# A graph layer's edge loop: shares of a column copy between ScalarE and VectorE, its rates, and where a row is added

## The chip, the cores and the metric

One core of a Trainium2 chip. The metric is the device time of one execution in microseconds (us). Engines are named as the profile names them: PE is TensorE (PEld its weight loads), DVE is VectorE, ACT is ScalarE, POOL is GpSimd, SP is the engine that issues most DMAs.

## What is computed

A message-passing layer over N = 12500 nodes with 64 features and E = 200000 edges with 32 features, a residual and a layer norm. Edges are sorted by destination, and low node numbers have many more edges than high ones.

```python
msg_in = concat([x[src], x[dst], edge_attr])            # 64 + 64 + 32
messages = relu(msg_in @ mW1 + mb1) @ mW2 + mb2          # hidden 128
aggregated = segment_sum(messages, dst, num_segments=N)
upd = relu(concat([x, aggregated]) @ uW1 + ub1) @ uW2 + ub2
out = layernorm(x + upd)
```

All of it is float32.

## The kernel before

**Tables.** The part of the first product that belongs to a node is computed once a node: `tab_a` holds x @ mW1[:64] and `tab_b` x @ mW1[64:128] + mb1, 128 numbers a node. An edge's hidden row is then the sum of a row of `tab_a` (its source), a row of `tab_b` (its destination) and a small product of its 32 features.

**Tiles and groups.** 128 edges make a tile, six tiles a group (`SUB = 6`): 1563 tiles, 261 groups, the last of three tiles. Two groups share their selection matrices (`SUP = 12`). The main loop runs over the groups `s` and writes each engine's order by hand; an engine works its own instructions off in that order and waits on semaphores for the others. In one pass of the loop stand, among others: `node_part(s)`, a first part of the DVE copies (`joined`), `collect(s - 1)`, in every other pass `select` (lines 257 and 263, the selection matrices) with another part of the copies, `edge_part(s + 1)`, the last part of the DVE copies, and the ACT copies (`singly`).

**What a group needs.**
- GpSimd gathers the source rows: one indirect DMA a tile (line 223) from `tab_a` into the tile `xg`. The first ten groups gather rows of `x` itself, which are transposed. `ROWB = 9` buffers let the gathers of a group start once a group nine places earlier has been added.
- PE computes the destinations' and the edge features' part into the PSUM tile `pc` (line 385, `edge_part`).
- DVE adds the gathered rows to `pc` (line 408; line 411 for the last, shorter group), and ACT applies the Relu, from `pc` into the SBUF tile `h` (line 409; 412).
- PE sums `h` by destination into the PSUM tile `sums` and counts edges into `cnt` (lines 444 and 441, `collect`).
- Some 480 nodes at a time are closed, updated, normalised and stored: lines 447 to 537, spread over several passes. `cps`, `y`, `ss`, `sd`, `hTu` and `pu` are their tiles.

**Copied groups.** A gather of one tile takes GpSimd as long as any other, so in some groups the last two tiles are not gathered. Their 256 source columns are copied instead, out of the transposed node features that lie in SBUF (`xtop` and `xbot`), as 128 columns of `xc`, each made of two halves; PE then multiplies `xc` with `w1a` into `pc` (line 388). `ACTS` of the 128 columns are copied by ACT (line 358, one instruction a column), the rest by DVE (line 365). The column's address is data, so each chunk of up to 8 columns is preceded by a load of its addresses into the engine's registers (line 334). `PACE` says how many copied groups are started for each group of the loop, by stage; the list `COPIED` follows from it, and so does the share of columns copied in each pass (`portion`). There are 107 copied groups, and a copied group's add covers four tiles of the six.

Of the kernel before, what the change touches and what calls it, by code (L numbers as in the profile page):

```python
# [12 lines left out]
AF = mybir.ActivationFunctionType  # L13
ALU = mybir.AluOpType
# [10 lines left out]
SUB = 6  # L25
# [45 lines left out]
U8 = mybir.dt.uint8  # L71
YBASE = XBASE + 4 * XCOLS
LEAD = 8
PACE = ((11, 0.435), (50, 0.458), (130, 0.438), (170, 0.425), (261, 0))
FINAL = 258


def progress(s):

    return sum(r * max(0, min(s + 1, b) - a) for (a, r), (b, _) in zip(PACE, PACE[1:]))  # L80


COPIED = []
# [1 line left out]
    while progress(s) >= len(COPIED) + 1 and s + 3 < FINAL:  # L85
        COPIED.append(s + 3)
LAST = 4 * (N - 1)
ACTS, CHUNK = 64, 8


def updates():
# [24 lines left out]
def gnn_kernel(ctx: ExitStack, tc: tile.TileContext, x1T, x, eT, e_rows, src, src_row, dst, dst_row, wlist, wrow, wnext, whalf,  # L116
# [24 lines left out]
    nc = tc.nc  # L141
# [64 lines left out]
    def tiles(s):  # L206
        return range(s * SUB, min((s + 1) * SUB, NT))
# [20 lines left out]
    with tc.tile_pool(name="sup", bufs=2) as sup, tc.tile_pool(name="work", bufs=2) as work, tc.manual_schedule():  # L228
# [140 lines left out]

        def parts(n):  # L370

            return [(slice(b, b + 1), (n - b + 1) // 2) for b in range(2) if n > b]

        def edge_part(s):
# [16 lines left out]
        def node_part(s):  # L391

            n = len(tiles(s))
            pc = pcs.pop(s)
            h = work.tile([P, 2, SUB // 2, DH], F32, name="h")
            if s < XG:
                xt = xs.pop(s)
                for i in range(n):
                    k, b = divmod(i, 2)
                    q = 64 * b  # L400
                    nc.tensor.matmul(pc[:, b, k, :], xt[q:q + 64, k, :], w1a[q:q + 64], start=False,
                                     stop=i + 2 >= n)
                nc.scalar.activation(h, pc, AF.Relu)
            else:
                a = xg.pop(s)[0].rearrange("p (b k) f -> p b k f", b=2)
                if n == SUB:
                    m = SUB // 2 - (s in COPIED)
                    nc.vector.tensor_tensor(pc[:, :, :m], pc[:, :, :m], a[:, :, :m], op=ALU.add)  # L408
                    nc.scalar.activation(h, pc, AF.Relu)  # L409
                for b, m in parts(n) if n < SUB else []:  # L410
                    nc.vector.tensor_tensor(pc[:, b, :m], pc[:, b, :m], a[:, b, :m], op=ALU.add)
                    nc.scalar.activation(h[:, b, :m], pc[:, b, :m], AF.Relu)
            hs[s] = h

        def opened(u):
# [359 lines left out]
        n = UPD[K - 1]  # L775
# [8 lines left out]
        for s in range(last + 2):  # L784
# [13 lines left out]
            if s < NSUB:  # L798
                node_part(s)
                joined(s, 0, 3 if j == 0 and g + 1 < NSUP else 2)  # L800
# [59 lines left out]
    with tc.If(flag > 0), tc.tile_pool(name="gen", bufs=1) as up:  # L860
# [28 lines left out]
        with tc.For_i(0, NT, 1) as t:  # L889
# [26 lines left out]
            pc = psum.tile([P, DH], F32, name="pcg", tag="pc")  # L916
# [4 lines left out]
            h = up.tile([P, DH], F32, name="hg")  # L921
# [6 lines left out]
            m = up.tile([P, 1], F32, name="m")  # L928
# [97 lines left out]
```

## Time and profile before

| | us |
|---|---|
| median of 3 runs | 1726.23 |
| lowest and highest | 1725.64, 1727.5 |
| the profiled execution | 1724.81 |
| its span, first to last instruction | 1723.0 |
| granted TensorE clock, mean | 0.582 of full speed |

Rows of a view that groups instructions read: line, engine, operation, written tile <- read tiles, shape and count, then busy time and mean duration in ns, then the idle time of the engine just before these instructions and what ended it. In a list of waits stand the total in us, the number of times and the longest. "issue" is idle time for which the profile shows no wait: the engine's own sequencer was at something else. In a row of a stage stand start:end, length, the busy time of each engine with its count of instructions, the granted clock, the DMA share and GB/s. A timeline row has its start, its duration, and in brackets the idle time before it.

### The profile page before, as it was taken

To read this page: it belongs to the slowest core of one execution; us is meant where nothing else is said; L and a number is where in the kernel's file an instruction comes from. 1 tells how busy PE (TensorE), PEld (TensorE's weight loads), DVE (VectorE), ACT (ScalarE), POOL (GpSimd) and SP (SyncE) were. 2 spreads that over 40 slices of the span, in tenths; PEclk is the share of its full clock that TensorE was granted. 3 is DMA by queue.
4 is the path that set the end of the run, shared out by engine and by line. 5 is a ranking of instruction groups with operands and counts; after the bars stand their busy time and mean duration, and the time that the engine had idled before them with its cause. 6 is when DMAs were issued, how large, how long until landed. Compare 5 with 4: busy or idle time off the path is not lost. (4 is left out here: it accounts for less than half of the span.)

```text
span 1723.0 us, 47177 instructions
## 1 busy us (share of the span) xinstructions
PE 1444.9 (84%) x9576; PEld 1251.9 (73%) x9608; DVE 1062.7 (62%) x7605; ACT 1555.2 (90%) x7279; POOL 1277.0 (74%) x1358
## 2 busy tenths in 40 slices
PE   2696888888878888888888988888887898999987
PEld 2585777787767777777776887776776677877776
DVE  1426666666666666666666666666666666666563
ACT  0176999999999999999999999999999999999892
POOL 7777777777777777777777777777777777777771
PEclk8575555556555555655565555556666656555576
DMA  8783433433333333333333333343333443334332
GB/s 208 202 182 99 118 109 111 125 101 93 94 95 97 92 101 94 98 102 96 105 98 108 108 109 106 104 112 110 108 104 107 112 111 109 110 107 111 105 108 63
DMA packets 205695, 190.92 MB, mean 111 GB/s; under 512 B 55938, under 2 KB 171862, under 8 KB 205414
## 3 DMA queue, kind: packets, MB, share of 16 engines
q1 hardware_dynamic: 147700, 92.42, 19.6%
q0 software_dynamic: 43168, 86.53, 18.4%
q10 hardware_dynamic: 14546, 8.93, 1.9%
q8 instruction: 91, 1.49, 0.3%
q14 instruction: 190, 1.55, 0.3%
HBM read 170.26 MB, written 17.47 MB: 109 GB/s over the span
## 5 line engine op out<-in xcount | busy, mean ns | idle before, releaser
L223 POOL DMA_INDIRECT xg<-tab_a,src_s x1289 | 1218.4, 945 | 393.1 <-issue 356.1
L358 ACT ACTIVATE xc<-xtop,xbot 128x1 f32 x6848 | 1299.2, 290 | 31.3 <-issue 21.4
L365 DVE TENSOR_TENSOR xc<-xtop,xbot 128x1 int32 x6848 | 584.7, 153 | 451.3 <-issue 440.2
L444 PE MATMUL sums<-sel,h 128*128 128x32 f32 x3126 | 642.9, 372 | 79.3 <-ACT h L409 78.4
L444 PEld LDWEIGHTS sums<-sel,h 128*128 128x128 f32 x3126 | 609.2, 296 | 104.4 <-ACT h L409 89.5
L385 PE MATMUL pc<-rhs,l 64*128 64x128 f32 x3126 | 421.0, 412 | 81.5 <-DVE tb L610 28.8
L385 PEld LDWEIGHTS pc<-rhs,l 64*128 64x128 f32 x3126 | 348.1, 289 | 145.4 <-issue 63.0
L408 DVE TENSOR_TENSOR pc<-pc,xg 128x768 f32<-128x768 f32 (+1 forms) x250 | 212.9, 852 | 76.9 <-PE pc L385 26.7
L409 ACT ACTIVATE h<-pc 128x768 f32<-128x768 f32 x250 | 200.3, 801 | 25.4 <-DVE pc L408 24.5
L257 DVE TENSOR_TENSOR l<-l,cps 128x768 f32<-128x768 int32 (+1 forms) x134 | 126.7, 945 | 28.9 <-DMA l<-in_dst_row 17.5
L441 PEld LDWEIGHTS <-one 128*1 128x1 bf16 x1563 | 57.6, 83 | 84.9 <-issue 74.8
L441 PE MATMUL cnt<-sel,one 128*1 128x32 bf16 x1563 | 94.3, 187 | 0.7 <-issue 0.5
L388 PE MATMUL pc<-w1a,xc 64*128 64x128 f32 x428 | 80.5, 384 | 0.0
L263 DVE TENSOR_TENSOR sel<-cps,drc 128x384 f32<-128x384 f32 x131 | 71.3, 545 | 12.6 <-PE sums L444 12.5
L223 POOL DMA_INDIRECT xg<-in_x,src_s x60 | 57.6, 959 | 19.1 <-issue 18.0
L388 PEld LDWEIGHTS pc<-w1a,xc 64*128 64x128 f32 x428 | 71.5, 298 | 0.0
L482 PE MATMUL pu<-xw,uz 128*128 128x480 f32 (+2 forms) x64 | 61.9, 1071 | 0.3 <-DVE xw L459 0.3
L602 ACT COPY tb<-pb 128x512 f32<-128x512 f32 (+1 forms) x13 | 7.4, 569 | 60.1 <-DMA tab_a<-tb 21.1
L439 PE MATMUL cnt<-zero_b 128*1 128x512 bf16 x32 | 18.5, 578 | 47.1 <-DVE xw L459 42.5
L483 PE MATMUL pu<-sums_s,w2u 128*128 128x480 f32 (+2 forms) x64 | 54.4, 952 | 0.0
L498 PE MATMUL cps<-ux,xw 128*128 128x64 f32 x244 | 45.7, 348 | 8.5 <-DVE sel L263 7.9
L498 PEld LDWEIGHTS cps<-ux,xw 128*128 128x128 f32 x244 | 41.0, 253 | 13.8 <-DVE sel L263 10.3
(111 smaller groups left out, 598.6 us busy)
## 6 DMA issues: line engine op xcount, KB each, us to landing
l<-in_dst_row SPq DMA_DIRECT2D x262, 96.0 KB
l<-in_eT SPq DMA_DIRECT2D x262, 96.0 KB
xg<-tab_a,src_s POOLq DMA_INDIRECT x1289
rhs<-tab_b SPq DMA_DIRECT2D x361, 32.0 KB
tab_b<-tb SPq DMA_DIRECT2D x13, 512.0 KB
rhs<-tab_b SPq DMA_DIRECT2D x387, 16.0 KB
tab_a<-tb ACTq DMA_DIRECT2D x12, 512.0 KB
out<-y SPq DMA_DIRECT2D x30, 128.0 KB
```

The source lines that it names most:

```text
L223: nc.gpsimd.indirect_dma_start(out=a[:, i, :] if s < XG else a[:, i // 2, i % 2, :], out_offset=None, in_=A[:, :] if s >= XG else x[:, :], ...
L257: nc.vector.tensor_tensor(l[r], l[r].bitcast(I32), node[r].unsqueeze(2).broadcast_to([r.stop - r.start, SUP // 2, P]), op=ALU.is_equal)
L263: nc.vector.tensor_tensor(s[:, :nt], slot.unsqueeze(1).broadcast_to([P, nt, WIN]), drc[:, g * SUP:g * SUP + nt].unsqueeze(2).broadcast_to( ...
L358: nc.scalar.activation(o[:, e:e + 1], top.bitcast(F32), AF.Identity, bias=bot.bitcast(F32))
L365: nc.vector.tensor_tensor(o[:, e:e + 1].bitcast(I32), top.bitcast(I32), bot.bitcast(I32), op=ALU.bitwise_or)
L385: nc.tensor.matmul(pc[:, b, k, :], L[g][q:q + 64, m, :], rhs[g % 2][q:q + 64, w, :], start=s >= XG or k == 0, stop=s >= XG and not copied)
L388: nc.tensor.matmul(pc[:, b, k, :], xc[s][q:q + 64], w1a[q:q + 64], start=False, stop=True)
L408: nc.vector.tensor_tensor(pc[:, :, :m], pc[:, :, :m], a[:, :, :m], op=ALU.add)
L409: nc.scalar.activation(h, pc, AF.Relu)
L441: nc.tensor.matmul(pn[:, bass.ds(ws[i], WIN)], one, SB[g][:, k0 + i, :, 1], start=False, stop=ends and i == n - 1)
L444: nc.tensor.matmul(ps[:, bass.ds(ws[i], WIN)], h[:, i % 2, i // 2, :], S[g][:, k0 + i, :], start=False, stop=ends and i == n - 1)
L498: nc.tensor.matmul(py[:, i], xw[u % 2][:, i * P:(i + 1) * P], ux, start=i == 0, stop=False)
```

## The change

Four edits. ACT copies 62 columns of a copied group where it copied 64, and DVE 66 where it copied 64. The four rates of `PACE` become 0.44, 0.462, 0.437 and 0.423 for 0.435, 0.458, 0.438 and 0.425; there are still 107 copied groups, some of them one group earlier. In groups that are not copied DVE writes the sum of `pc` and the gathered rows into `h` in SBUF, and ACT applies the Relu to `h` in place, where the sum was written back to `pc` in PSUM and the Relu read it there; the last, shorter group likewise. Copied groups keep the add in PSUM.

```diff
-PACE = ((11, 0.435), (50, 0.458), (130, 0.438), (170, 0.425), (261, 0))
+PACE = ((11, 0.44), (50, 0.462), (130, 0.437), (170, 0.423), (261, 0))
...
-ACTS, CHUNK = 64, 8
+ACTS, CHUNK = 62, 8
...
         def parts(n):
 
+            if n == SUB:
+                return [(slice(0, 2), SUB // 2)]
             return [(slice(b, b + 1), (n - b + 1) // 2) for b in range(2) if n > b]
...
-                if n == SUB:
-                    m = SUB // 2 - (s in COPIED)
+                if s in COPIED:
+                    m = SUB // 2 - 1
                     nc.vector.tensor_tensor(pc[:, :, :m], pc[:, :, :m], a[:, :, :m], op=ALU.add)
                     nc.scalar.activation(h, pc, AF.Relu)
-                for b, m in parts(n) if n < SUB else []:
-                    nc.vector.tensor_tensor(pc[:, b, :m], pc[:, b, :m], a[:, b, :m], op=ALU.add)
-                    nc.scalar.activation(h[:, b, :m], pc[:, b, :m], AF.Relu)
+                for b, m in parts(n) if s not in COPIED else []:
+                    nc.vector.tensor_tensor(h[:, b, :m], pc[:, b, :m], a[:, b, :m], op=ALU.add)
+                    nc.scalar.activation(h[:, b, :m], h[:, b, :m], AF.Relu)
```

## The prediction

> **What bounds the kernel now.** I read the page's first part, then the waits of GpSimd, then the timelines of GpSimd and VectorE side by side, then busy time by stage, and last the waits inside each stage.
>
> ```profile
> span 1723.0 us, 47177 instructions
> ...
> PE 1444.9 (84%) x9576; PEld 1251.9 (73%) x9608; DVE 1062.7 (62%) x7605; ACT 1555.2 (90%) x7279; POOL 1277.0 (74%) x1358
> ```
>
> By shares ACT looks like the bound and VectorE (DVE) like an idle engine. Both readings need a second view. GpSimd first:
>
> ```profile
> POOL xg L223 <- issue: 374.0, 1227, 0.3
> ```
> ```profile
> 1510.31 0.94 POOL L223 DMA_INDIRECT xg<-tab_a,src_s  x1 [0.30 <-issue]
> ...
> 1688.95 0.94 POOL L223 DMA_INDIRECT xg<-tab_a,src_s  x1 [0.30 <-issue]
> ```
> ```profile
> 1527.28 0.97 DVE L408 TENSOR_TENSOR pc<-pc,xg 128x768 f32<-128x768 f32 x1 [1.89 <-DMA xg<-tab_a,src_s]
> ...
> 1710.29 0.43 DVE L411 TENSOR_TENSOR pc<-pc,xg 128x256 f32<-128x256 f32 x1 [2.48 <-PE pc L385]
> ```
>
> No gap of GpSimd is longer than the 0.3 us between two gathers, so it is never held up by a buffer: a gather every 1.25 us (0.94 + 0.30), the last started at 1688.95. The change keeps 107 copied groups, so 1349 gathers, and this end stays. It is a floor, not the bound: counting gathers, the row at 1510.31 is the last of group 232, whose rows are added only at 1527.28, and group 260's, from 1688.95, at 1710.29. The consumers run 17 to 21 us behind the gathers, and whatever they save moves the end, up to some 15 us; what they lose moves it without limit. 12.7 us after 1710.29 the span ends.
>
> So which consumer? Busy time in five stages (core 0: PE, PEld, DVE, ACT, POOL), the adds of line 408 in the middle three, and the waits within them:
>
> ```profile
> 120.00:385.00 265.00, 216.82 (x1473) 197.81 (x1470) 174.06 (x1212) 237.45 (x1119) 200.38 (x213) 0.51 0.40 111
> 385.00:900.00 515.00, 432.70 (x2781) 380.68 (x2786) 334.27 (x2572) 511.76 (x2496) 389.42 (x413) 0.55 0.34 97
> 900.00:1125.00 225.00, 201.39 (x1231) 174.19 (x1236) 148.10 (x1108) 222.28 (x1067) 170.13 (x181) 0.54 0.38 107
> 1125.00:1520.00 395.00, 341.87 (x2298) 287.55 (x2307) 260.52 (x1901) 385.78 (x1837) 298.63 (x317) 0.63 0.40 109
> 1520.00:1711.00 191.00, 174.84 (x1127) 144.17 (x1134) 109.33 (x729) 156.28 (x713) 128.42 (x136) 0.62 0.37 103
> ```
> ```profile
> 120.00:385.00 265.00, 34.84 (x41) 0.51 0.40 111
> 385.00:900.00 515.00, 68.86 (x82) 0.55 0.34 97
> 900.00:1125.00 225.00, 30.79 (x36) 0.54 0.38 107
> 1125.00:1520.00 395.00, 53.73 (x64) 0.63 0.40 109
> ```
>
> The four waits of DVE in 120:385, 385:900, 900:1125 and 1125:1520, in that order:
>
> ```profile
> DVE xc L365 <- issue: 66.1, 119, 1.6
> ```
> ```profile
> DVE xc L365 <- issue: 163.6, 314, 1.4
> DVE pc L408 <- PE pc L388: 3.3, 3, 1.8
> DVE l L257 <- ACT y L507: 3.1, 4, 0.9
> DVE pc L408 <- PE pc L385: 2.8, 2, 1.9
> ```
> ```profile
> DVE xc L365 <- issue: 63.7, 132, 1.1
> DVE pc L408 <- PE pc L388: 4.3, 3, 1.8
> DVE pc L408 <- PE pc L385: 3.4, 3, 1.9
> ```
> ```profile
> DVE xc L365 <- issue: 107.7, 216, 1.1
> DVE pc L408 <- PE pc L388: 6.1, 4, 1.7
> DVE pc L408 <- PE pc L385: 5.3, 6, 1.5
> DVE l L257 <- ACT y L507: 5.3, 8, 1.0
> ```
>
> ACT is busy 511.76 of 515 us in the second stage and 222.28 of 225 in the third: it is the bound there. But DVE's "issue" is not rest. It is the time in which its sequencer loads column addresses into registers before a chunk of copies (line 334), and nothing else runs on that queue meanwhile. With it DVE is taken for 334.27 + 163.6 = 497.9 of 515 us (97%), 211.8 of 225 (94%) and 260.52 + 107.7 = 368.2 of 395 (93%). The kernel stands balanced on two engines, and the change takes from the one and gives to the other.
>
> **The price of one column.**
>
> ```profile
> 722.21 0.65 DVE L365 TENSOR_TENSOR xc<-xtop,xbot 128x1 int32 x8 [0.51 <-issue]
> 723.68 0.65 DVE L365 TENSOR_TENSOR xc<-xtop,xbot 128x1 int32 x8 [0.81 <-issue]
> 725.14 0.70 DVE L365 TENSOR_TENSOR xc<-xtop,xbot 128x1 int32 x8 [0.81 <-issue]
> ```
> ```profile
> L334 DVEq TENSOR_LOAD <-col_a x1037: 342/1102/2403, 124.3 to 1679.9; - x173
> ```
> ```profile
> 703.20 5.66 ACT L358 ACTIVATE xc<-xtop,xbot 128x1 f32 x30
> ```
>
> On DVE chunks of 8 columns follow each other every 1.465 us (722.21 to 725.14 over two), of which a load takes 1.10: 0.183 us a column, not the 0.08 that the busy time (0.65 for 8) suggests. On ACT 30 copies take 5.66 us; less the 0.29 of the last one that is 0.185 us a column, the loads hidden under the copies. So the trade is one for one: 214 columns fewer on ACT are 39.6 us, 214 more on DVE 39.2 us. In the instruction order of the two programs DVE has 1040 address loads for 1037, ACT 991 for 1006: no new chunks, only fuller ones.
>
> **By stage**, with the rates of the diff (columns a group on DVE: 0.462 x 66 - 0.458 x 64 = +1.18 in groups 50 to 129, and so on; on ACT 0.462 x 62 - 0.458 x 64 = -0.67):
> - 120:385, 41 groups: DVE +1.20 each, 49 columns, +9.0 us on 174.06 + 66.1 = 240.2 of 265. It fits, but this stage is full of stalls; bounds 0 and +9, I take +2.
> - 385:900, 82 groups: DVE +97 columns, +17.7: 497.9 + 17.7 = 515.6. ACT falls by 55 columns, 10.2 us. DVE is now full. If all its waits for PE and ACT vanish the stage grows by 0.6 us; if the 9.2 quoted stay, by 9.8. They follow node updates, whose work on PE and ACT stays, so I take +8.
> - 900:1125, 36 groups: DVE +0.81 each, +5.3: 217.1; with its 7.7 of waits 224.8. ACT 222.28 - 6.3 + 0.8 (below) = 216.8. Between -7.9 and -0.2; nearer the DVE row, -1.
> - 1125:1520, 64 groups: DVE +0.72 each, +8.4: 376.6, with 16.7 of waits 393.3. ACT 385.78 - 11.5 + 1.4 = 375.7. Between -18 and -1.7; -3.
> - 1520:1711: PE is busy 174.84 of 191 and the last add quoted waits for PE. Copies end here; 0, bounds -4 and +2.
>
> The rates also move which groups are copied: in the middle the same number of copied groups is reached one group earlier, so a gather starts up to 2.5 us (two gathers of 1.25) earlier, and none at the end. GpSimd does not bound: 0.
>
> **The add and the Relu in SBUF.** 143 groups change (250 full groups less 107 copied).
>
> ```profile
> L409 ACT ACTIVATE h<-pc 128x768 f32<-128x768 f32 x250 | 200.3, 801 | 25.4 <-DVE pc L408 24.5 <-ACT xc L358 0.2
> L585 ACT ACTIVATE xbot<-ident 64x1568 f32<-64x1568 f32 x8 | 12.1, 1510 | 0.1
> L507 ACT ACTIVATE y<-cps 128x256 f32<-128x256 f32 x30 | 11.2, 375 | 0.1
> ```
> ```profile
> L408 DVE TENSOR_TENSOR pc<-pc,xg 128x768 f32<-128x768 f32 x143 | 138.2, 966 | 42.5 <-PE pc L385 25.0 <-DMA xg<-tab_a,src_s 5.2 <-issue 2.8
> L610 DVE TENSOR_TENSOR tb<-pb,b 128x1024 f32<-128x1024 f32 x12 | 14.5, 1212 | 16.0 <-PE pb L592 16.0
> ```
>
> From PSUM a Relu costs (801 - 375) / 512 = 0.83 ns an element and 162 ns fixed; line 585, from SBUF, 1510 - 1568 x 0.83 = 205 ns fixed. So 43 ns more for each of the 143 (it doesn't show a Relu of SBUF): 6.1 us of ACT in all, 0.02 a group, in the sums above. [...]
>
> The add: from 256 to 768 elements it grows from 0.43 to 0.966 us, 1.05 ns an element. Line 610, PSUM to SBUF, has 1212 - 1024 x 1.05 = 137 ns beside that, line 408 966 - 768 x 1.05 = 160. So -23 ns at best, and I count nothing: the next address load starts with the add and lasts longer (1.10 against 0.97). If that cover went, it would be -3.3 us. New waits: the add now needs the h of two groups before to have been read; those matmuls stand ahead of this group's pc on PE, for which the add waits anyhow: nothing. PSUM is free after the add rather than the Relu, which can give back at most
>
> ```profile
> PEld pc L385 <- ACT h L409: 6.0, 4, 1.8
> ```
>
> 6.0 us, on an engine that does not bound the early stages: 0.
>
> **Sum:** +2 + 8 - 1 - 3 = +6 us. The profiled execution took 1724.81 us (1723.0 of span and 1.8 around it), so 1730.8; on the median of 1726.23, which is 1.4 above it, 1732.2.
>
> **The rivals.**
> - Faster: ACT alone decides, and DVE takes its new columns out of its waits. Then the stages give their lower ends, 0, +0.6, -7.9, -18; the gathers allow only some 14 of that (17 less about 3 for landing, an estimate from the lags), and PE, at 87% in 1125:1520, less. For it: ACT's 99% and so few waits of ACT. Against: DVE's 97% in 385:900. It decides once the waits of DVE shrink by half in 900:1520. -10 us, 1716. Chance 0.29.
> - All waits stay and the first stage, too, pays in full: +9 + 9.8 - 0.2 - 1.7 = +17, 1743. Chance 0.12.
> - The trade is even: within 0.2% (3.45 us, about what a measurement of this kernel tells from no change), 1726. Chance 0.13; what DVE loses by 900 us is then regained after 900 as the rates fall.
>
> My forecast, DVE the bound up to 900 us and little regained, has 0.46, with its own range of 1730 to 1738. Slower is 0.46 + 0.12 = 0.58, the same 0.13, faster 0.29. For 8 in 10 I reach to 1715 and 1744, past the times of both outer cases by a microsecond.
>
> **What would show it.** Right: in 385:900 DVE's busy time and issue fill the stage, ACT's share falls from 99% to about 97% with new waits "ACT h <- DVE", fewer groups are added by 900 us, and the lag at group 232 is over 17 us. The Relu of SBUF takes 830 to 860 ns; copies cost the same each. Wrong: ACT still at 99% in 385:900, or the lag at 232 below 12 us, or GpSimd with waits for buffers, which would make the loss larger.

## The result, and the profile after

| | us |
|---|---|
| kernel before, median of 6 runs | 1726.87 (1724.6 to 1730.07) |
| changed kernel, median of 6 runs | 1738.54 (1735.54 to 1741.96) |
| ratio | 1.0068, 95% interval 1.0052 to 1.0083 |
| profiled execution of the changed kernel | 1735.54, of which the span is 1733.8 |

The change makes the kernel 11.7 us slower, where 6.0 us were forecast. Between the two profiled executions the difference is 10.7 us (1735.54 - 1724.81).

First DVE's copies in the kernel before; then the changed kernel's page: its span, the busy time of each engine, and the same group. Then, from the view that keeps shapes apart, the add and the Relu in SBUF and the Relu that still reads PSUM (these line numbers stand two higher than before).

```profile
L365 DVE TENSOR_TENSOR xc<-xtop,xbot 128x1 int32 x6848 | 584.7, 153 | 451.3 <-issue 440.2
```
```profile
span 1733.8 us, 47215 instructions
...
PE 1450.5 (84%) x9608; PEld 1242.8 (72%) x9608; DVE 1075.6 (62%) x7819; ACT 1531.5 (88%) x7065; POOL 1277.1 (74%) x1358
...
L365 DVE TENSOR_TENSOR xc<-xtop,xbot 128x1 int32 x7062 | 601.2, 154 | 485.8 <-issue 474.3
```
```profile
L413 DVE TENSOR_TENSOR h<-pc,xg 128x768 f32<-128x768 f32 x143 | 136.9, 957 | 29.8 <-PE pc L387 19.3 <-DMA xg<-tab_a,src_s 2.6 <-issue 1.5
L414 ACT ACTIVATE h<-h 128x768 f32<-128x768 f32 x143 | 119.7, 837 | 38.3 <-DVE h L413 37.1
L411 ACT ACTIVATE h<-pc 128x768 f32<-128x768 f32 x107 | 84.8, 793 | 9.1 <-DVE pc L410 8.5 <-ACT xc L358 0.2
```

ACT is busy 23.7 us less (1555.2 to 1531.5), DVE only 12.9 us more, and still the span grew by 10.8. Now the same five stages as before (the first is left out), in the columns PE, PEld, DVE, ACT, POOL:

```profile
385.00:900.00 515.00, 426.41 (x2705) 370.35 (x2704) 331.54 (x2609) 497.55 (x2381) 389.38 (x413) 0.54 0.36 96
900.00:1125.00 225.00, 197.39 (x1271) 170.06 (x1270) 148.75 (x1131) 216.23 (x1032) 169.83 (x180) 0.57 0.40 106
1125.00:1520.00 395.00, 345.93 (x2283) 286.94 (x2283) 261.99 (x1935) 376.18 (x1766) 298.71 (x317) 0.61 0.41 109
1520.00:1711.00 191.00, 175.97 (x1146) 142.93 (x1145) 116.50 (x795) 160.95 (x728) 128.64 (x137) 0.64 0.40 105
```

The waits of DVE and of ACT in 385:900 (total, times, longest):

```profile
DVE xc L365 <- issue: 171.0, 303, 1.2
DVE h L413 <- PE pc L387: 2.9, 4, 0.9
```
```profile
ACT xc L358 <- issue: 9.6, 34, 0.4
ACT h L414 <- DVE h L413: 6.5, 12, 0.9
```

ACT fell from 511.76 of 515 us (99%) to 497.55 (97%) and waits more for the sums that DVE makes (6.5 us). DVE is taken for 331.54 + 171.0 = 502.5 (98%; 497.9 before). The groups' passage shows what that costs. These are the adds of groups 48, 128 and 168 in the kernel before, then of groups 48, 128, 168, 232 and 260 in the changed one (start, duration):

```profile
373.32 0.70 DVE L408 TENSOR_TENSOR pc<-pc,xg 128x512 f32<-128x512 f32 x1
...
878.07 0.97 DVE L408 TENSOR_TENSOR pc<-pc,xg 128x768 f32<-128x768 f32 x1
...
1127.55 0.70 DVE L408 TENSOR_TENSOR pc<-pc,xg 128x512 f32<-128x512 f32 x1
```
```profile
372.20 0.70 DVE L410 TENSOR_TENSOR pc<-pc,xg 128x512 f32<-128x512 f32 x1
...
889.52 0.70 DVE L410 TENSOR_TENSOR pc<-pc,xg 128x512 f32<-128x512 f32 x1 [0.34 <-issue]
...
1138.87 0.96 DVE L413 TENSOR_TENSOR h<-pc,xg 128x768 f32<-128x768 f32 x1 [0.15 <-PE pc L387]
...
1541.50 0.96 DVE L413 TENSOR_TENSOR h<-pc,xg 128x768 f32<-128x768 f32 x1 [1.09 <-PE pc L387]
...
1720.10 0.62 DVE L413 TENSOR_TENSOR h<-pc,xg 128x256 f32<-128x256 f32 x2 [3.30 <-PE pc L387]
```

From group 48 to 128 the changed kernel takes 517.3 us for 504.8: there the loss is made. From 128 to 168 it takes the same (249.4 for 249.5), to 232 2.9 us more (402.6 for 399.7), to 260 4.4 less (178.6 for 183.0). GpSimd's last gather of group 232 and its last of all:

```profile
1510.38 0.94 POOL L223 DMA_INDIRECT xg<-tab_a,src_s  x1 [0.30 <-issue]
...
1689.14 0.94 POOL L223 DMA_INDIRECT xg<-tab_a,src_s  x1 [0.31 <-issue]
```

They start when they did before (1510.31 and 1688.95). Behind them the consumers lag 31.1 us at group 232 (17.0 before) and 31.0 at group 260 (21.3).

### The profile page after: what moved, and what is told of

It is laid out like the page before. It is cut to its first block, busy times and chain, and to the rows that moved or that the text cites. A ratio compares the mean times of both kernels' runs of the same rounds, so it can differ in the third digit from the quotient of the medians.

```text
span 1733.8 us, 47215 instructions
## 1 busy us (share of the span) xinstructions
PE 1450.5 (84%) x9608; PEld 1242.8 (72%) x9608; DVE 1075.6 (62%) x7819; ACT 1531.5 (88%) x7065; POOL 1277.1 (74%) x1358
## 5 line engine op out<-in xcount | busy, mean ns | idle before, releaser
L358 ACT ACTIVATE xc<-xtop,xbot 128x1 f32 x6634 | 1258.4, 281 | 45.5 <-issue 36.5
L365 DVE TENSOR_TENSOR xc<-xtop,xbot 128x1 int32 x7062 | 601.2, 154 | 485.8 <-issue 474.3
L413 DVE TENSOR_TENSOR h<-pc,xg 128x768 f32<-128x768 f32 (+1 forms) x145 | 137.5, 949 | 33.1 <-PE pc L387 22.6
L414 ACT ACTIVATE h<-h 128x768 f32<-128x768 f32 (+1 forms) x145 | 120.3, 830 | 42.8 <-DVE h L413 41.6
L411 ACT ACTIVATE h<-pc 128x768 f32<-128x768 f32 x107 | 84.8, 793 | 9.1 <-DVE pc L410 8.5
L410 DVE TENSOR_TENSOR pc<-pc,xg 128x512 f32<-128x512 f32 x107 | 74.7, 698 | 16.8 <-PE pc L390 10.6
L390 PE MATMUL pc<-w1a,xc 64*128 64x128 f32 x428 | 84.7, 387 | 0.0
L390 PEld LDWEIGHTS pc<-w1a,xc 64*128 64x128 f32 x428 | 75.7, 302 | 0.0
L223 POOL DMA_INDIRECT xg<-in_x,src_s x60 | 57.5, 959 | 19.1 <-issue 17.7
```

Of the source, the lines that this page charges most:

```text
L223: nc.gpsimd.indirect_dma_start(out=a[:, i, :] if s < XG else a[:, i // 2, i % 2, :], out_offset=None, in_=A[:, :] if s >= XG else x[:, :], ...
L358: nc.scalar.activation(o[:, e:e + 1], top.bitcast(F32), AF.Identity, bias=bot.bitcast(F32))
L365: nc.vector.tensor_tensor(o[:, e:e + 1].bitcast(I32), top.bitcast(I32), bot.bitcast(I32), op=ALU.bitwise_or)
L390: nc.tensor.matmul(pc[:, b, k, :], xc[s][q:q + 64], w1a[q:q + 64], start=False, stop=True)
L413: nc.vector.tensor_tensor(h[:, b, :m], pc[:, b, :m], a[:, b, :m], op=ALU.add)
L414: nc.scalar.activation(h[:, b, :m], h[:, b, :m], AF.Relu)
```

## The experiments

Theories on record: A, DVE is what the changed kernel waits for, through its new columns; B, the Relu that reads SBUF costs ACT the time; C, the rates do. In eight of the runs the kernel before took about 2470 us, too (the last section shows one of their traces); they are told at the end of this section and settle nothing about 1726 us.

**Two columns fewer on ACT.** The changed kernel, with

```diff
-            todo = [(o, k, e) for o, k, lo, hi in portion(s, ACTS) for e in range(lo, hi, 2)]
+            todo = [(o, k, e) for o, k, lo, hi in portion(s, ACTS - 2) for e in range(lo, hi, 2)]
...
+                    w = 3 if e == ACTS - 3 else 1
+                    nc.scalar.activation(o[:, e:e + w], top.bitcast(F32).broadcast_to([P, w]), AF.Identity,
+                                         bias=bot.bitcast(F32))
```

> The changed kernel, but ACT leaves 2 of its 62 columns out of every copied group (its last copy writes 3 columns with one value, so the output isn't the reference's): 2 x 0.185 us x 107 = 39.6 us less work on ACT, none less on DVE. Theory A (DVE is what the changed kernel waits for, through its 66 columns): the time stays within 2 us of the changed kernel's, 1.005 to 1.008 of the kernel before. Theory B (ACT is still what it waits for, through the Relu that reads SBUF): the time falls by 8 us or more below the changed kernel's, to 1.002 of the kernel before or less. Theory C (the rates): as A, 1.005 to 1.008.

Measured: 1740.03 us, ratio 1.007 (1.0046 to 1.0094), within 1.5 us of the changed kernel. 385:900 and ACT's first two waits in it:

```profile
385.00:900.00 515.00, 425.18 (x2688) 372.57 (x2694) 333.61 (x2619) 488.43 (x2321) 388.10 (x411) 0.54 0.36 96
```
```profile
ACT xc L359 <- issue: 13.6, 45, 0.6
ACT h L416 <- DVE h L415: 10.3, 19, 1.1
```

ACT has 26.6 us free in 515 and it buys nothing. Theory B falls for the changed kernel: what its Relu costs ACT lies in time that ACT has to spare.

**Two columns fewer on DVE.** The mirror image.

```diff
-            todo = [(o, k, ACTS + e) for o, k, lo, hi in portion(s, P - ACTS) for e in range(lo, hi, 2)]
+            todo = [(o, k, ACTS + e) for o, k, lo, hi in portion(s, P - ACTS - 2) for e in range(lo, hi, 2)]
...
+                    w = 3 if e == P - 3 else 1
+                    nc.vector.tensor_tensor(o[:, e:e + w].bitcast(I32), top.bitcast(I32).broadcast_to([P, w]),
+                                            bot.bitcast(I32).broadcast_to([P, w]), op=ALU.bitwise_or)
```

> The changed kernel, but DVE leaves 2 of its 66 columns out of every copied group (its last copy writes 3 columns with one value, so the output isn't the reference's): 2 x 0.183 us x 107 = 39.2 us less work on DVE, none less on ACT. Theory A (DVE is what the changed kernel waits for): 8 us or more come back, 0.995 to 1.002 of the kernel before. Theory B (ACT through the Relu that reads SBUF, or the two engines through their hand-over of the sum): at most 3 us come back, 1.005 to 1.008. Theory C (the rates): as B.

Measured: 1711.97 us, ratio 0.9904 (0.9881 to 0.9928), beyond what A expected: 15 us below the kernel before and 27 below the changed one, for 39.2 us of DVE. The last gather and the add of group 260:

```profile
1690.53 0.94 POOL L223 DMA_INDIRECT xg<-tab_a,src_s  x1 [0.30 <-issue]
```
```profile
1697.91 0.62 DVE L414 TENSOR_TENSOR h<-pc,xg 128x256 f32<-128x256 f32 x2 [2.45 <-PE pc L388]
```

The lag is 7.4 us where it was 31.0: the consumers have nearly caught up with the gathers, which leaves little of the 39.2 us to be had beyond the 27. 385:900 in this run, with DVE's first wait in it:

```profile
385.00:900.00 515.00, 435.55 (x2789) 381.01 (x2788) 334.79 (x2585) 505.25 (x2436) 389.42 (x413) 0.54 0.37 97
```
```profile
DVE xc L366 <- issue: 165.6, 310, 1.3
```

DVE is still taken for 500.4 us (97%), so that share alone does not tell which engine decides; the pair of runs does. The same run says something of the kernel before. It has as many DVE copies as that one and 39.6 us fewer on ACT, less some 6 for the Relu, and is 15 us faster. That points to ACT's copies costing time, too, at 64 and 64, though the run has the new rates and the sums in SBUF as well, so this is not shown.

**The columns alone.** The kernel before, with

```diff
-ACTS, CHUNK = 64, 8
+ACTS, CHUNK = 62, 8
```

> The kernel before with the columns alone: ACT copies 62 and DVE 66 of a copied group; old rates, sums in PSUM. Taking 2 columns off DVE has brought the changed kernel from 1.0070 to 0.9904 and taking 2 off ACT has brought nothing, so the bound is DVE. Theory A1 (the columns that the change gave DVE make the whole loss): 8 to 13 us over the kernel before, 1.005 to 1.0075. Theory A2 (the columns load DVE, but the Relu that reads SBUF or the rates make over half of the loss): 1.000 to 1.003. Theory A3 (the columns cost more than the change lost, and the sums in SBUF give some back): 1.008 or more.

Measured: 1746.16 us, ratio 1.01 (1.0071 to 1.0129): 17 us by the ratio, 20 by the medians, and A3 is nearest. The interval overlaps that of the whole change (1.0052 to 1.0083), so whether the other two edits give some 5 us back is not settled. The adds of groups 48, 128, 168, 232 and 260:

```profile
377.96 0.70 DVE L408 TENSOR_TENSOR pc<-pc,xg 128x512 f32<-128x512 f32 x1
...
890.97 0.97 DVE L408 TENSOR_TENSOR pc<-pc,xg 128x768 f32<-128x768 f32 x1
...
1142.22 0.70 DVE L408 TENSOR_TENSOR pc<-pc,xg 128x512 f32<-128x512 f32 x1
...
1550.31 0.97 DVE L408 TENSOR_TENSOR pc<-pc,xg 128x768 f32<-128x768 f32 x1 [1.03 <-PE pc L385]
...
1734.49 0.43 DVE L411 TENSOR_TENSOR pc<-pc,xg 128x256 f32<-128x256 f32 x1 [2.48 <-PE pc L385]
```

Each column below gives the us from add to add, from one profiled execution a kernel. The run with two columns fewer on ACT has the changed kernel's work on DVE, so its distance from the changed kernel shows how well a stretch repeats: to 5 us in the first, to 1.5 or better in the others. The profiled execution of the columns alone took 1748.53 us, 2.4 above their median.

| groups | before | changed | two fewer on ACT | columns alone | DVE copies before, changed, columns alone |
|---|---|---|---|---|---|
| up to 48 | 373.3 | 372.2 | 377.4 | 378.0 | 1030, 1074, 1062 |
| 48 to 128 | 504.8 | 517.3 | 515.8 | 513.0 | 2342, 2436, 2414 |
| 128 to 168 | 249.5 | 249.4 | 249.7 | 251.3 | 1122, 1156, 1160 |
| 168 to 232 | 399.7 | 402.6 | 402.8 | 408.1 | 1744, 1790, 1796 |
| 232 to 260 | 183.0 | 178.6 | 179.3 | 184.2 | 610, 606, 630 |

(The copies are counted from `PACE` and `portion` over the passes of a stretch; the rates spread a copied group's columns over several passes.) The columns alone cost in every stretch: 4.6, 8.3, 1.8, 8.4 and 1.2 us. From 168 to 232 the whole change loses only 2.9 us with nearly as many copies, 1790 for 1796, so fewer copies are not the reason. That leaves the new rates or the sums in SBUF; the runs do not say which.

**One copied group fewer.** If both copying engines hold the kernel before and GpSimd has room, one copied group fewer, for two gathers more, should help. The kernel before, with

```diff
-PACE = ((11, 0.435), (50, 0.458), (130, 0.438), (170, 0.425), (261, 0))
+PACE = ((11, 0.4306), (50, 0.4534), (130, 0.4336), (170, 0.4208), (261, 0))
```

> The kernel before with every rate times 0.99 (0.4306, 0.4534, 0.4336, 0.4208): 106 copied groups for 107, so 64 copies (11.8 us) fewer on ACT, 64 copies with their address loads (11.7 us) fewer on DVE, and 2 gathers (2.5 us) more on GpSimd. The sum over the last group starts 21 us after the last gather in the kernel before and 7 us after it where DVE has 39.2 us less to do. Theory A (the two copying engines, near to even at 64 and 64, set the end, GpSimd has 14 us to spare): about 11 us less, 0.992 to 0.996. Theory D (only the engine that is relieved by itself counts and the other one holds the gain): 0.998 to 1.001. Theory E (the gathers are the floor after all): 2.5 us more, 1.001 to 1.003.

Measured: 1717.12 us, ratio 0.9939 (0.9918 to 0.996): as theory A expected; D and E are ruled out. The run does not tell the two engines apart, since it relieves both by as much: if DVE alone held the kernel before, its 11.7 us would bring the same. The last gather and the add of group 260:

```profile
1691.28 0.94 POOL L223 DMA_INDIRECT xg<-tab_a,src_s  x1 [0.31 <-issue]
```
```profile
1702.88 0.43 DVE L411 TENSOR_TENSOR pc<-pc,xg 128x256 f32<-128x256 f32 x1 [3.34 <-PE pc L385]
```

The last gather starts 2.3 us later, the last add 7.4 us earlier, and the lag is 11.6 us. This version computes all of the reference and beats both kernels.

**The eight runs at 2470 us.** The columns alone, three times:

> The kernel before with one part of the change: ACT copies 62 and DVE 66 columns; rates and adds as before. Theory A (DVE is the bound once it has more columns): with 0.9 columns a group more at 0.183 us each the stage 385 to 900 us, where DVE had 17 us of 515 left, grows by about 8, and little comes back later: +5 to +9 us on the time before. Theory B (the Relu that reads SBUF costs the time, on ACT): ACT is relieved by 39 us and nothing else changes, so -5 to 0. Theory C (the rates): 0.

> The kernel before with one part of the change: ACT copies 62 and DVE 66 columns; rates and adds as before. [...] Theory A: +5 to +9 us on the time before. Theory B: -5 to 0. Theory C: 0.

> The kernel before with the columns alone: ACT copies 62 and DVE 66 of a copied group; old rates, sums in PSUM. Theory A (DVE, through its columns, makes the loss): 8 to 12 us over the kernel before, 1.005 to 1.007. Theory B (the SBUF Relu on ACT makes it): 0.997 to 1.001, since ACT gets 39.6 us less to do. Theory C (the rates): 0.998 to 1.002.

Ratios 0.9993 (0.9964 to 1.0021), 1.0041 (1.0011 to 1.0071) and 1.0012 (0.9982 to 1.0041). The sums in SBUF alone, twice (the last two hunks of the change, without the columns and the rates):

> The kernel before with one part of the change: adds and Relus of groups that are not copied in SBUF; 64 columns each and the old rates. Theory A: ACT, still the bound here, pays 143 times some 36 to 43 ns, 5 to 6 us in all, and up to 2.9 us of DVE come back: +2 to +6. Theory B: the whole slowdown, +10 to +12. Theory C: 0.

> The kernel before with the sums alone changed: a group that isn't copied is added in SBUF and its Relu reads SBUF; 64 and 64 columns, old rates. The columns alone have cost 1.010 (1.0071 to 1.0129), the whole change 1.0068 (1.0052 to 1.0083). Theory A3 (sums in SBUF or the rates give 5 us back, PSUM being free earlier): 0.995 to 0.999. Theory B (the Relu that reads SBUF costs ACT 143 x 0.043 = 6 us, which the columns' relief of ACT hides in the whole change, and which shows here, where ACT is 99% busy): 1.002 to 1.004. Neither: 0.999 to 1.002.

Ratios 1.0038 (1.0007 to 1.0069) and 1.0033 (1.0001 to 1.0065), some 9 us and the same twice. The rates alone (the first hunk), the changed kernel with 64 and 64 columns, and the changed kernel with two columns fewer on DVE:

> The kernel before with one part of the change: the new rates; 64 columns each, adds in PSUM. Theory A: 0.26 columns a group more on both engines between groups 50 and 129, about 0.05 us a group or 4 us by group 130, given back by the lower rates later: 0 to +3. Theory B: 0. Theory C: the whole slowdown, +10 to +12.

> The changed kernel with 64 columns on each engine again (new rates and SBUF adds stay). Theory A: the part of the columns goes, so 4 to 8 us faster than the changed kernel, +3 to +7 on the time before. Theory B: as slow as the changed kernel or slower, +11 to +20, since ACT has its 39 us back. Theory C: +10 to +12, as the changed kernel.

> The changed kernel, but DVE copies 64 of its 66 columns: the last two are left out (one copy writes the same column three times, so these two columns are wrong); ACT still copies 62. Theory A (DVE is the bound): 214 copies at 0.183 us, 39 us of DVE, go; ACT becomes the bound again, with 62 columns, and the gathers are next: 10 to 18 us faster than the changed kernel, -7 to +1 on the time before. Theory B (the Relu that reads SBUF, on ACT): ACT's work is as in the changed kernel, so +10 to +12 stay. Theory C (the rates as such): +10 to +12 stay, less a little.

Ratios 1.0074 (1.0043 to 1.0104), 1.0146 (1.0103 to 1.0188) and 1.0166 (1.0099 to 1.0233). That they belong to another balance is seen from the last: the program that is 15 us below the kernel before at 1726 us stands here 41 us above it. So the price of the sums in SBUF alone, and of the rates alone, at 1726 us stays open.

## Why the prediction was right, point by point

The direction and the engine were right. The size was half of what came, 6.0 us for 11.7, and 1738.54 lies just past the upper end of the forecast's own range (1738) and about midway between the forecast's 1732.2 and the rival "all waits stay" (1743). In the three middle stretches the miss is larger: +4 forecast (8 - 1 - 3), 15.4 measured (12.6 - 0.1 + 2.9).

- **DVE, not ACT, decides.** Shown for the changed kernel, by the pair of runs: 39.6 us off ACT bring nothing, 39.2 us off DVE bring 27. The reading that carried it was to count "issue" as taken time; by the busy shares (DVE 62%, ACT 88%) one would guess the opposite. The signs it named are there: DVE 98% taken in 385:900, ACT at 97% with more waits for line 413, 36 + 43 = 79 groups added in that stage for 82,

```profile
385.00:900.00 515.00, 25.08 (x36) 0.54 0.36 96
```
```profile
385.00:900.00 515.00, 41.17 (x43) 0.54 0.36 96
```

  and a lag of 31.1 us at group 232. GpSimd waits for DVE's line 413 in gaps of at most 0.7 us, 3.4 us in all. (The kernel before, too, had a few gaps over 0.3: up to 0.5, and one of 1.1 for the source numbers.)

```profile
POOL xg L223 <- issue: 380.3, 1248, 0.3
...
POOL xg L223 <- DVE h L413: 3.4, 10, 0.7
```

- **The price of a column** holds nearly. Busy time and "issue" before the copies make 1502.9 us of DVE in the kernel before (1062.7 + 440.2) and 1549.9 in the changed one (1075.6 + 474.3): 47.0 us for the 39.2 forecast. A DVE copy takes 154 ns for 153 and the address loads are as many and as long as forecast; ACT's copies show 281 ns for 290. That "nothing else runs on that queue meanwhile" was wrong: of the 990 us of loads in the kernel before some 630 lie beside an instruction of DVE that is at work, and only the rest in idle time. Behind another chunk 0.81 us of idle time is left of a load, behind an add 0.51 (the rows at 723.68 and 722.21), so the price was that of chunk behind chunk.

```profile
L334 DVEq TENSOR_LOAD <-col_a x1040: 340/1104/2417, 120.8 to 1684.5; - x174
```

- **385:900, +8.** Mis-sized: group 48 to 128 takes 12.6 us more, above the bound of 9.8, and 11.1 more in the run with two columns fewer on ACT. In these groups DVE is taken for 488.7 us before and 505.0 after, 16.3 more, near the 17.7 forecast. What failed is the room: 16.1 us were left before, 12.3 are left after, so 3.8 of the new work went into waits where 9.7 were forecast to. The kernel before:

```profile
373.32:878.07 504.75, 423.33 (x2701) 374.22 (x2708) 328.86 (x2530) 502.06 (x2451) 381.61 (x405) 0.54 0.34 97
```
```profile
DVE xc L365 <- issue: 159.8, 308, 1.4
```

  and the changed one:

```profile
372.20:889.52 517.32, 425.06 (x2694) 370.42 (x2691) 333.84 (x2625) 499.82 (x2394) 391.16 (x415) 0.54 0.36 96
```
```profile
DVE xc L365 <- issue: 171.2, 303, 1.2
```

- **900:1125, -1.** The time is about right: -0.1 from group 128 to 168. There 7.1 us more of DVE's work went into its waits (235.0 to 242.1 us taken), where 6.3 were forecast to.
- **1125:1520, -3.** The step that failed in its sign: +2.9 from group 168 to 232. DVE is taken for 11.6 us more (370.9 to 382.5), where 8.4 were forecast, and 8.7 us of its 28.8 us of room went, where 11.4 were forecast to. Before and after:

```profile
1127.55:1527.28 399.73, 346.62 (x2320) 292.64 (x2330) 262.50 (x1917) 390.32 (x1858) 302.15 (x321) 0.62 0.40 109
```
```profile
DVE xc L365 <- issue: 108.4, 218, 1.1
```
```profile
1138.87:1541.50 402.63, 352.20 (x2336) 293.54 (x2331) 265.43 (x1963) 382.14 (x1793) 304.30 (x323) 0.61 0.41 109
```
```profile
DVE xc L365 <- issue: 117.1, 238, 1.2
```

- **The bounds.** They set DVE's busy time, issue and listed waits against the stage's length, though in the kernel before itself these make only 260.52 + 107.7 + 16.7 = 384.9 of 395 us, and 507.1 of 515 in 385:900. The rest (in 1125:1520 3.7 us in shorter rows of the list and 6.4 in gaps below what it shows) was counted as room. Set against its own stage first, "all waits stay" would have read +17.7 and +8.4 there, not +9.8 and -1.7. The measured +12.6 and +2.9 lie below those: part of the waits went, as forecast, but a smaller part.
- **The start and the end, +2 and 0.** -1.1 up to group 48 and -4.4 from 232 on: these two hid part of the miss above, which is luck. The start does not repeat (+4.0 in the run with two columns fewer on ACT); the end does (-3.8). The runs do not say which edit gives it.
- **The rates, 0.** For the gathers it holds: the last one starts at 1689.14 for 1688.95. What the rates do to DVE was in the stages' sums. They put 22 copies more, 4.0 us, into groups 48 to 128 than the columns alone have, and 24 fewer, 4.4 us, from 232 on; the changed kernel is 4.3 us slower than the columns alone there and 5.6 faster here. That fits, but no run with the rates alone at 1726 us shows it.
- **The Relu in SBUF, +43 ns.** Measured 837 ns: 36 more than the 801 of the kernel before, 44 more than the changed kernel's own Relu from PSUM (793), so 5 to 6 us in all. The forecast's 43 was an estimate from three rows of the kernel before (801 ns of line 409, 375 of line 507, 1510 of line 585). The time does not hang on it, since ACT has room: 39.6 us less work there brought nothing.
- **The add in SBUF, at best -23 ns.** Measured 957 for 966, -9 ns, or 1.3 us over 143 adds.
- **The rivals.** "ACT alone decides" falls by the pair of runs. "All waits stay", 1743, is near what the columns alone do (1746.16); the whole change lies between it and the forecast.

## What to carry to other kernels

DVE, which loads addresses before small copies, was busy for 62% of the span and taken for 97 to 98% of 385:900. Count such an engine's "issue" time, and check that busy time, issue and waits make up the stage's length in the kernel before, before what is missing there is counted as room. Where two engines share one job and both are near full, moving work from one to the other can lose, as here (the columns alone took 1746.16 us for 1726.54): look for a third that has room, as GpSimd had here for two more gathers (1717.12 us for 1726.47). To find the engine that decides, take the same amount of work from each in turn: one run brought nothing and its mirror image 27 us.

## What the runs showed of the hardware

**The clock and the time.** The granted TensorE clock differs from one execution to the next, and the time with it. Of the 46 executions of the kernel before that stood beside the four sets of runs at 1726 us, the 15 at a clock of 0.585 or more (0.586 on average) took 1725.1 us, the 15 at 0.579 or less (0.578) 1731.3. So PE may have a part in the time, which no run here takes apart. In each of the four sets the mean clocks of the two kernels lie within 0.006 of each other; by these averages an estimate of what that can make is 5 us at most.

**Idle time without a wait.** The same program ran at two speeds. The columns alone took 1746.16 us in one set of runs and 2467.5 in another, and the kernel before beside them 1726.54 and 2468.4. Two groups of the page of the slower one, and then of the faster one:

```profile
L223 POOL DMA_INDIRECT xg<-tab_a,src_s x1289 | 1216.8, 944 | 1105.8 <-DVE pc L408 644.1
L358 ACT ACTIVATE xc<-xtop,xbot 128x1 f32 x6634 | 1304.3, 282 | 330.9 <-issue 309.6
```
```profile
L223 POOL DMA_INDIRECT xg<-tab_a,src_s x1289 | 1218.7, 945 | 393.7 <-issue 362.1
L358 ACT ACTIVATE xc<-xtop,xbot 128x1 f32 x6634 | 1259.9, 282 | 52.2 <-issue 41.4
```

Each of these instructions takes as long (944 and 945, 282 and 282 ns). What differs is the idle time ahead of them. On ACT's copies 309.6 us of it, for 41.4, show no wait, in stretches where copies come in ones and twos; DVE in the slower run:

```profile
707.80 0.23 DVE L365 TENSOR_TENSOR xc<-xtop,xbot 128x1 int32 x2 [0.73 <-issue]
708.51 0.16 DVE L365 TENSOR_TENSOR xc<-xtop,xbot 128x1 int32 x1 [0.49 <-issue]
709.22 0.23 DVE L365 TENSOR_TENSOR xc<-xtop,xbot 128x1 int32 x2 [0.55 <-issue]
```

In these rows the groups start at steps of 0.71 us. GpSimd, which waits for DVE in gaps of at most 0.3 us in 385:900 of the faster run, waits 644.1 us for line 408 in the whole of the slower one (143.0 of them in 385:900, 8.5 at the longest). It is not one chip against another: on the chip that the record numbers 14 the kernel before took 1727 us in one set and 2468 in the next. Where this idle time comes from is not in these traces and stays open.
